# A hybrid eight-layer kernel: sparse experts whose first products run before the gate's weights, and an attention norm placed earlier in the pipeline

## The chip, the cores and the metric

The kernel runs on one core of a Trainium2 chip. A core has a matrix engine (TensorE, PE in the profile; its weight loads are PEld), a vector engine (VectorE, DVE), an engine for activation functions (ScalarE, ACT), a general one (GpSimd, POOL) and an engine that issues transfers (SyncE, SP). They run their own instruction streams in order and meet at semaphores. The metric is the device time of one execution in microseconds (us); lower is better. Times of three runs are given by their median.

## The reference

The model takes `x` of 4 batches, 1024 positions and 128 features, in float32, and applies eight layers, each to the normalised input, and each added to it:

```
x = x + _L0_attn_a_ref(_layernorm(x), ...)
x = x + _L0_ffn_ref(_layernorm(x), ...)       # sparse experts, call 1
x = x + _L0_attn_b_ref(_layernorm(x), ...)
x = x + _L0_ffn_ref(_layernorm(x), ...)       # sparse experts, call 2
x = x + _L1_attn_a_ref(_layernorm(x), ...)
x = x + _L1_ffn_ref(_layernorm(x), ...)
x = x + _L1_attn_b_ref(_layernorm(x), ...)    # multi-query attention
x = x + _L1_ffn_ref(_layernorm(x), ...)
```

Two of these matter here. The sparse experts have 8 experts of 128 hidden units, of which each token uses the best two, and a shared one that every token uses:

```
logits = einsum('btd,ed->bte', x, gate_w)
_, idx = top_k(logits + lb_bias, 2)
w = sigmoid(logits at idx);  w = w / (sum(w) + 1e-6)
we = w placed at idx, 0 elsewhere                        # token x expert
hidden = square(relu(einsum('nd,ehd->neh', x, w1)))
moe_out = sum over e of we * (hidden_e @ w2_e)
shared = square(relu(x @ cfc)) @ cproj
return moe_out + shared
```

The multi-query attention has 16 heads of 64, which share one key and one value head. Each head has a bias that depends on the distance between positions; the scores are causal:

```
q = (x @ Wq) * 64**-0.5;  k, v = x @ Wkv
sim = q k^T + 8 * rel_emb[bucket(distance)], masked above the diagonal
out = softmax(sim) v;  return out @ Wout + bout
```

## The kernel before

The stream `x_sb` stays in SBUF for the whole kernel, 128 positions to a tile, 8 tiles to a batch. Layers follow one another, and a scheduler puts the instructions of each engine in order, by their dependences and their place in the program; an inner `manual_schedule` fixes the written order for the engines it names. In the experts that is PE alone; in the multi-query attention it is PE, DVE and ACT. Work that a later layer may begin early (its norms, for instance) can be woven into the DVE and ACT streams of the layer before it.

**Sparse experts (`ffn0`, called twice).** The two batches at work at any time are objects of the class `Batch`. Its constructor normalises the batch (`layernorm`, lines 344 to 351); `turn` (L1042, L1043) transposes it on PE into `xT`; `gate` (L1019, L1050 to L1071) makes the logits on PE, and then on ACT and DVE the rank of each expert among the eight, and the weights `we` of the two best. Their square roots are taken (L1071), because the root is multiplied in ahead of the square: the square of `root * relu(h)` is `we * relu(h)^2`. Hidden units lie on partitions, so the root of each token must be the same on all 128 of them. `spread` brings this about: a transpose on PE (L1077), a copy (L1079), a write of the 64 x 128 roots to DRAM (L1081), and 16 loads that read one row into all partitions (L1087), one for each of 8 experts in each of two blocks of 512 tokens. The tile of roots has two buffers, one per block.

A `Block` is 512 tokens. `first(n)` makes the product with the first weights of one expert in a PSUM bank (L1099, two records in the trace for each matmul, with 512 columns). For the shared expert ACT rectifies it (L1102). For the other eight one DVE instruction takes the maximum with 0 and multiplies by the roots, straight from PSUM (L1105). ACT then squares the result in SBUF (L1106). `second(n)` issues a ninth of the 36 products with the second weights (L1115), which add up over the nine experts in one PSUM bank; after the ninth piece DVE adds the bank to the stream (L1124). The order on PE is that of the loop at the end of `ffn0`: for each block, nine times a `first` of this block and a `second` of the block before. The next batch is turned and gated after the seventh piece of a batch's first block, and spread after the fifth piece of its second block. There are six banks for first products, transposes and logits, and two for sums.

**Multi-query attention (`attn3`).** The loop runs over steps `s`. Each pair of heads has six steps, which take the query tiles 0 and 1, 2 and 3, 4, 5, 6, 7; a batch has eight pairs, so 48 steps. In a step, PE transposes the probabilities of the present step (L1962), makes the scores two steps ahead (L1912), which DVE biases (L1930), and ACT takes the exponentials one step ahead (L1947); then PE contracts the probabilities of the step before with the values (L1980), and after the fourth and the last tile DVE multiplies by the inverted sums (L1989). Between the two halves of the exponentials a step runs its `extras`: functions that were registered for it by `at(step, f)`. The preparation of the next batch is a list of seven such pieces, `batch.pieces`: two of statistics (`stats`, L1821 and L1822, on DVE), `scale` (a square root on ACT, L1829, which needs another function table than the exponentials, and the norm itself on POOL, L1833, eight tiles, and a bias on POOL, L1836), `turn` (L1845), `reverse` (L1852: the same tiles with the positions flipped), `keys` (L1859) and `values` (L1865). With `s` the first step of the new batch, piece `j` runs at step `s - 16 + j`: the statistics at the third and fourth step of a pair (steps are counted from 0 below, so these are steps 2 and 3), `scale` at step 4, `turn` at step 5, `reverse`, `keys` and `values` at steps 0, 1 and 2 of the next pair.

Of the kernel before, what the change touches and what calls it, by code (L numbers as in the profile page):

```python
# [29 lines left out]
AF = mybir.ActivationFunctionType  # L30
ALU = mybir.AluOpType
# [4 lines left out]
B, S, D, H = 4, 1024, 128, 16  # L36
P = 128
# [210 lines left out]
def hybrid_kernel(ctx: ExitStack, tc: tile.TileContext, x, out, blocks, dram, upto=8):  # L248
    nc = tc.nc
    mm = nc.tensor.matmul  # L250
# [32 lines left out]
    def layer_pool(name, bufs, side="left"):  # L283

        return tc.tile_pool(name=name, bufs=bufs, side=side, reuse_waits="tile")

    psum = Psum()
    bank, pair = psum.single, psum.pair
# [19 lines left out]
    early = wpool.tile([P, wide1], F32, name="wt1")  # L308
# [23 lines left out]
    after = const.tile([P, P], BF16, name="after")  # L332
# [689 lines left out]
    def ffn0(W):  # L1022

        E = 8
        with layer_pool("f0", 2, "right") as pool:

            class Batch:  # L1030
# [14 lines left out]
                def gate(self):  # L1045


                    lg = gate_logits(self.xT, W("gate"))
                    sg = small.tile([P, TB, E], F32, name="sg")
                    nc.scalar.activation(sg, lg, AF.Sigmoid)  # L1050
                    v = small.tile([P, TB, E], F32, name="v")
                    nc.vector.tensor_tensor(v, lg, wide(W("lb"), TB), ALU.add)
                    other = v.unsqueeze(2).to_broadcast([P, TB, E, E])
                    own = v.unsqueeze(3).to_broadcast([P, TB, E, E])
                    more = pool.tile([P, TB, E, E], F32, name="more", bufs=1)
                    same = pool.tile([P, TB, E, E], F32, name="same", bufs=1)
                    nc.vector.tensor_tensor(more, other, own, ALU.is_gt)
# [31 lines left out]
            class Block:  # L1089


                def __init__(self, batch, i):
                    self.batch, self.i = batch, i
                    self.hid = pool.tile([P, E + 1, 512], F32, name="hid")

                def first(self, n):
                    e = (n + E) % (E + 1)
                    ps = bank()
                    mm(ps, W("w1")[:, e * P : (e + 1) * P], self.batch.xT[:, self.i * 512 : (self.i + 1) * 512], start=True, stop=True)  # L1099
                    h = self.hid[:, e, :]  # L1100
                    if e == E:
                        nc.scalar.activation(h, ps, AF.Relu)  # L1102
                    else:
                        root = self.batch.root[self.i][:, e].rearrange("p t c -> p (t c)")
                        nc.vector.scalar_tensor_tensor(h, ps, 0.0, root, ALU.max, ALU.mult)  # L1105
                    nc.scalar.activation(h, h, AF.Square)  # L1106
# [19 lines left out]
            with tc.manual_schedule(engines={mybir.EngineType.PE}):  # L1126
                batch = Batch(0)
                batch.turn()
                batch.gate()
                batch.spread()  # L1130
                before = None
                for b in range(B):
                    for i in range(2):
                        block = Block(batch, i)
                        if i == 0 and b + 1 < B:
                            after = Batch(b + 1)
                        for n in range(E + 1):
                            block.first(n)
                            if before:
                                before.second(n)  # L1140
                            if i == 0 and n == 6 and b + 1 < B:
                                after.turn()
                                after.gate()
                            if i == 1 and n == 4 and b + 1 < B:
                                after.spread()
                        before = block
                    if b + 1 < B:
                        batch = after
                for n in range(E + 1):
                    before.second(n)  # L1150

# [634 lines left out]
    def attn3(W, table):  # L1786
# [9 lines left out]
        with layer_pool("a3", 2) as pool, layer_pool("a3k", 1) as keep:  # L1796
# [6 lines left out]
            def at(step, f):  # L1803
                extras.setdefault(step, []).append(f)
# [205 lines left out]
            for k, p in enumerate(pairs):  # L2010
                s = N * k
                for i in range(2):
                    at(s + 1 + 4 * i, lambda p=p, i=i: p.invert(i))
                    at(s + 2 + 4 * i, lambda p=p, i=i: p.spread(i))
                if k:
                    at(s - 5, p.fetch)
                    at(s - 4, p.project)
                if p.hp == 0 and k:
                    for j, piece in enumerate(p.batch.pieces):
                        at(s - 16 + j, piece)  # L2020
                if p.hp == 7:
                    for j, t0 in enumerate((0, 2)):
                        at(s + 4 + j, lambda p=p, t0=t0: p.batch.output(t0))
                        at(s + N + 1 + j, lambda p=p, t0=t0: p.batch.output(t0 + 4))
            engines = mybir.EngineType
            with tc.manual_schedule(engines={engines.PE, engines.DVE, engines.Activation}):
# [4 lines left out]
                before = None  # L2031
                for s in range(-2, total + 3):
                    p, step = (pairs[s // N], s % N) if 0 <= s < total else (None, 0)
# [18 lines left out]
                    before = (p, turned) if p else None  # L2052
# [43 lines left out]
```

## Time and profile before

| | us |
|---|---|
| median of three runs | 3670.81 (3669.97 to 3672.02) |
| the profiled execution, its own time | 3671.56 |
| its span in the trace | 3669.9 |
| experts, call 1, from its first transposes to its last second product | 920.5 to 1078.5 |
| experts, call 2, likewise | 1390.9 to 1547.1 |
| multi-query attention, from its first flips to its last output product | 2317.6 to 3424.8 |

The span is what lies between the first and the last instruction in the trace; the execution's own time has 1.66 us more around it. The page lists for each engine the time in which it was busy. A long busy share of PE does not mean that it works at its peak: its records also last longer when its clock is granted at half rate, and the page gives this clock by slices. The page's second part shows the clock below full in the first half of the kernel above all (tenths, 40 slices of 91.7 us):

```profile
PE   6999999998899998999989999999999998999999
PEclk7999999999899998989999999999999999999999
```

The trace can be asked for the instructions in a stretch in order of time, each with the idle time of its engine ahead of it and the instruction that ended this idle time. That is the view for a stretch with a few waits in it; sums over the whole span hide them.

### The profile page before, as it was taken

Reading aid. Unit: us, or ns where it says so; the run is one execution under the profiler, and the core shown is the slowest. Engines: PE = TensorE matmul, PEld = TensorE weight load, DVE = VectorE, ACT = ScalarE, POOL = GpSimd, SP = SyncE. Lnnn points to the kernel's source line nnn. Section 1 sums busy time; section 2 is a strip of 40 time slices with the busy share of each in tenths; the row PEclk is TensorE's granted clock in tenths of the full one; section 3 lists DMA queues with packets and bytes.
Section 4 is the critical chain, followed back from the end, with each engine's and each line's share of the span. In section 5 each row is a group of like instructions: output and inputs, shape, how many; then the busy total and the mean of one; then the engine's idle time right before and its main releaser. Section 6 shows DMA issues by size and latency. Waiting matters only on the chain.

```text
span 3669.9 us, 62785 instructions
## 1 busy us (share of the span) xinstructions
PE 3474.5 (95%) x25672; PEld 2046.2 (56%) x25672; DVE 2068.1 (56%) x4938; ACT 1961.9 (53%) x3349; POOL 919.0 (25%) x706
## 2 busy tenths in 40 slices
PE   6999999998899998999989999999999998999999
PEld 3344444435574556633333477666766766766777
DVE  5666666666653445468778621466566566566311
ACT  5455555556432223367767654466566566566543
POOL 4677777783004210122221100001001001000000
PEclk7999999999899998989999999999999999999999
DMA  3111111100430003400000000111001001010000
GB/s 99 46 47 47 47 47 47 47 24 1 139 87 1 1 1 108 116 1 1 1 1 1 14 1 1 61 34 36 27 33 36 28 32 35 24 36 24 4 9 13
DMA packets 95978, 124.36 MB, mean 34 GB/s; under 512 B 3660, under 2 KB 78028, under 8 KB 94536
## 3 DMA queue, kind: packets, MB, share of 16 engines
q1 hardware_dynamic: 95688, 120.33, 10.7%
q8 instruction: 202, 3.31, 0.4%
q14 instruction: 88, 0.72, 0.1%
HBM read 117.59 MB, written 2.73 MB: 33 GB/s over the span
## 4 chain that ended last, share of the span: by engine, by line
PE 83%; DVE 7%; ACT 6%; POOL 2%; issue 1%; DMA 1%; SPq 0%; ACTq 0%; DVEq 0%; POOLq 0%
PE mm L1962 8%; PE s L1912 8%; PE av L1749 6%; PE mm L1739 6%; PE av L1980 6%; PE s L734 5%; PE s L701 4%; PE s L1584 4%; PE av L772 3%; PE av L1115 3%; PE mm L1099 3%; PE av L1618 3%; ACT p L1947 2%; DVE p L1595 2%; PE mm L1288 2%; PE av L1324 2%
## 5 line engine op out<-in xcount | busy, mean ns | idle before, releaser
L764 POOL TENSOR_TENSOR p<-p,bias 128x1536 f32<-128x1536 f32 x192 | 504.3, 2627 | 89.0 <-ACT p L746 78.3
L1930 DVE CUSTOM_DVE_ANT_0 p<-s,bias 128x512 f32<-128x512 f32 (+3 forms) x768 | 387.2, 550 | 131.2 <-PE s L1912 123.9
L715 DVE TENSOR_REDUCE parts<-s 128x2 f32<-128x1024 f32 (+4 forms) x384 | 350.0, 953 | 151.5 <-PE s L701 90.6
L1947 ACT ACTIVATE p<-p,tops 128x128 f32<-128x128 f32 (+7 forms) x512 | 395.2, 774 | 2.7 <-DVE tops L1930 1.9
L1595 DVE TENSOR_SCALAR p<-s 128x1024 f32<-128x1024 f32 (+1 forms) x320 | 340.8, 1111 | 92.8 <-PE s L1584 83.5
L1967 ACT COPY pt<-mm 128x512 f32<-128x512 f32 (+1 forms) x352 | 185.8, 528 | 369.1 <-PE mm L1962 369.0
L1962 PE MATMUL mm<-ident,p 128*128 128x128 f32 x2304 | 348.7, 284 | 36.3 <-ACT p L1947 32.5
L1962 PEld LDWEIGHTS mm<-ident,p 128*128 128x128 f32 x2304 | 249.6, 141 | 173.4 <-issue 64.7
L1598 ACT ACTIVATE p<-p 128x2048 f32<-128x2048 f32 (+1 forms) x160 | 277.6, 1740 | 96.4 <-DVE p L1595 95.8
L1749 PEld LDWEIGHTS av<-wt,hid 128*128 128x128 f32 x2048 | 263.9, 192 | 107.1 <-issue 107.1
L1995 POOL COPY wide_rec<-rec 128x512 f32<-128x512 f32 x64 | 39.4, 616 | 1121.1 <-DVE rec L1993 1118.6
L1912 PE MATMUL s<-keys,q 64*128 64x512 f32 (+3 forms) x1536 | 303.6, 514 | 4.0 <-DVE tops L1930 4.0
L743 ACT ACTIVATE p<-s 128x1024 f32<-128x1024 f32 x192 | 155.7, 811 | 271.2 <-PE s L734 264.9
L1980 PE MATMUL av<-pt,vals 128*64 128x128 f32 x4608 | 295.1, 277 | 0.0
L1740 ACT ACTIVATE hid<-mm,wt 128x512 f32<-128x512 f32 x256 | 170.7, 690 | 220.8 <-PE mm L1739 220.5
L1980 PEld LDWEIGHTS av<-pt,vals 128*64 128x64 f32 x4608 | 248.8, 137 | 49.6 <-issue 38.5
L1749 PE MATMUL av<-wt,hid 128*128 128x128 f32 x2048 | 264.7, 275 | 0.0
L1739 PE MATMUL mm<-xT,wt 128*128 128x512 f32 x512 | 261.8, 602 | 2.5 <-ACT hid L1740 2.0
L1969 DVE COPY pt<-mm 128x512 f32<-128x512 f32 (+1 forms) x288 | 189.6, 658 | 131.8 <-PE mm L1962 131.7
L734 PE MATMUL s<-q,k 32*128 32x512 f32 (+3 forms) x1536 | 227.9, 537 | 0.5 <-DVE parts L715 0.5
L1584 PE MATMUL s<-q,k 32*128 32x512 f32 (+3 forms) x1536 | 213.5, 542 | 2.1 <-DVE p L1595 1.7
L701 PE MATMUL s<-k,q 32*128 32x512 f32 (+3 forms) x1280 | 180.3, 513 | 10.3 <-DVE parts L715 6.9
(400 smaller groups left out, 5281.0 us busy)
## 6 DMA issues: line engine op xcount, KB each, us to landing
root<-roots SPq DMA_DIRECT2D x128, 256.0 KB, 6.4
bias<-rel_dram SPq DMA_DIRECT2D x32, 1024.0 KB, 5.5
bias<-pos_dram SPq DMA_DIRECT2D x16, 1536.0 KB, 7.0
bias<-pos_dram SPq DMA_DIRECT2D x16, 512.0 KB, 7.9
wt<-w_ffn SPq DMA_DIRECT2D x2, 2132.0 KB, 8.1
wt<-w_ffn SPq DMA_DIRECT2D x2, 1192.0 KB, 5.3
wt<-w_attn SPq DMA_DIRECT2D x1, 2336.0 KB
x_sb<-x SPq DMA_DIRECT2D x4, 512.0 KB, 6.9
```

What stands on the lines that cost most here:

```text
L715: nc.vector.tensor_reduce(o, x, AX.X, ALU.max, negate=True)
L734: mm(both[h // 2][:, h % 2, 0:w], self.k[jt // 4][r, (3 - jt % 4) * P : (4 - jt % 4) * P], self.q[i][r, w0:512], start=True, stop=True,)
L764: nc.gpsimd.tensor_tensor(d, d, self.bias[:, 0:3, u : u + w], ALU.mult)
L1584: mm(both[h // 2][:, h % 2, c : c + 512 - w0], self.k[r, jt * P : (jt + 1) * P], self.q[r, 512 * i + w0 : 512 * (i + 1)], start=True, stop ...
L1595: nc.vector.tensor_scalar(pt[:, 2 * hp : 2 * hp + 2, 0:w], both[hp][:, :, 0:w], 80.0, -80.0, ALU.min, ALU.max)
L1739: mm(ps, W("w1")[:, c * P : (c + 1) * P], self.batch.xT[:, self.i * 512 : (self.i + 1) * 512], start=True, stop=True)
L1749: mm(o, self.hid[:, c, t * P : (t + 1) * P], W("w2")[:, c * P : (c + 1) * P], start=(c == 0), stop=(c == C - 1))
L1912: mm(s[:, kk, 0:e], self.q[r, it * P : (it + 1) * P], keys[self.n][r, S - n + c : S - n + c + e], start=True, stop=True,)
L1930: nc.vector.tensor_tensor_reduce(out=self.p[it][:, kk, c : c + e], in0=s[:, kk, 0:e], in1=self.bias[:, kk, c : c + e], scale=-1.0, scalar= ...
L1947: nc.scalar.activation(p, p, AF.Exp, bias=self.top[it][:, kk : kk + 1], scale=-1.0, accum_out=self.sums[:, it, kk : kk + 1])
L1962: nc.tensor.transpose(ps[:, m, kk, :], self.p[it][:, kk, (m0 + m) * P : (m0 + m + 1) * P], ident)
L1980: mm(self.acc[64 * kk : 64 * kk + 64, (it % 4) * P : (it % 4 + 1) * P], vals[self.n][:, it - m0 - m, :], pt[:, m, kk, :], start=(m0 + m == 0),
```

## The change

Two things are changed.

In `ffn0` the first batch's 18 first products (two blocks of nine) get their own two functions. `early` makes the product and rectifies it on ACT, for all nine experts, without roots. `weigh` multiplies the eight experts' results by the roots in SBUF, on DVE, and squares them on ACT. The written order becomes: turn and gate the first batch; nine `early` of block 0; `spread`; nine `early` of block 1; turn and gate the second batch; `weigh` all of both blocks; the 36 second products of block 0, now with no first products between them; `spread` of the second batch. From the second batch on the loop is that of before, with the second block of the first batch as the block before.

In `attn3` the seven pieces run at steps `s` less 21, 20, 19, 13, 11, 9 and 8 instead of 16 to 10. The statistics and `scale` are thus five steps earlier (steps 3, 4 and 5 of an earlier pair), `turn` stays, and `reverse`, `keys` and `values` come at steps 1, 3 and 4 of the pair in which they were at 0, 1 and 2.

The operations of every other layer, and their order on each engine, are as before. So is the number of instructions on PE, DVE, POOL and SP; ACT has 32 more, 16 in each call of `ffn0`.

```diff
+                def early(self, n):
+
+                    e = (n + E) % (E + 1)
+                    ps = bank()
+                    mm(ps, W("w1")[:, e * P : (e + 1) * P], self.batch.xT[:, self.i * 512 : (self.i + 1) * 512], start=True, stop=True)
+                    nc.scalar.activation(self.hid[:, e, :], ps, AF.Relu)
+
+                def weigh(self, n):
+                    e = (n + E) % (E + 1)
+                    h = self.hid[:, e, :]
+                    if e < E:
+                        root = self.batch.root[self.i][:, e].rearrange("p t c -> p (t c)")
+                        nc.vector.tensor_tensor(h, h, root, ALU.mult)
+                    nc.scalar.activation(h, h, AF.Square)
+
...
                 batch.gate()
-                batch.spread()
-                before = None
-                for b in range(B):
+                early = [Block(batch, i) for i in range(2)]
+                for i in range(2):
+                    for n in range(E + 1):
+                        early[i].early(n)
+                    if i == 0:
+                        batch.spread()
+                after = Batch(1)
+                after.turn()
+                after.gate()
+                for i in range(2):
+                    for n in range(E + 1):
+                        early[i].weigh(n)
+                for n in range(E + 1):
+                    early[0].second(n)
+                after.spread()
+                before = early[1]
+                for b in range(1, B):
+                    batch = after
                     for i in range(2):
...
                             block.first(n)
-                            if before:
-                                before.second(n)
+                            before.second(n)
...
                 if p.hp == 0 and k:
-                    for j, piece in enumerate(p.batch.pieces):
-                        at(s - 16 + j, piece)
+
+                    for j, piece in zip((21, 20, 19, 13, 11, 9, 8), p.batch.pieces):
+                        at(s - j, piece)
```

More of the change, by code (lines that the diff above doesn't have):

```diff
@@ L1146, in ffn0 @@
                         before = block
-                    if b + 1 < B:
-                        batch = after
                 for n in range(E + 1):
```

## Prediction

> **What bounds the kernel now.** I read the page first: one engine holds the span.
>
> ```profile
> span 3669.9 us, 62785 instructions
> PE 3474.5 (95%) x25672; PEld 2046.2 (56%) x25672; DVE 2068.1 (56%) x4938; ACT 1961.9 (53%) x3349; POOL 919.0 (25%) x706
> root<-roots SPq DMA_DIRECT2D x128, 256.0 KB, 6.4
> ```
>
> TensorE (PE) is busy 95%. The change issues every matmul of before and no other, so it can win only where PE stands still or runs at a reduced clock. I then read the timeline at the head of both expert layers (calls 1 and 2) and at the three places in the multi-query layer where the next batch is prepared. Head of call 1 (columns: start, length, engine, line, operands; in brackets the idle time before and its releaser):
>
> ```profile
> 922.60 3.50 PE L1019 MATMUL mm<-wt,xT 128*128 128x8 f32 x16
> 932.23 0.26 ACT L1071 ACTIVATE we<-we 128x64 f32<-128x64 f32 x1 [4.35 <-DVE we L1070]
> 932.54 0.42 PE L1077 MATMUL mm<-ident,we 128*64 128x128 f32 x1 [6.44 <-ACT we L1071]
> 932.76 7.92 PE L1099 MATMUL mm<-xT,wt 128*128 128x512 f32 x14
> 935.18 16.27 SPq L1087 DMA_DIRECT2D root<-roots  x16
> 940.27 1.53 DVE L1105 SCALAR_TENSOR_TENSOR hid<-mm,root 128x512 f32<-128x512 f32 x2 [5.49 <-DMA root<-roots]
> ...
> 969.12 1.02 PE L1099 MATMUL mm<-xT,wt 128*128 128x512 f32 x2
> ```
>
> PE ends the gate logits at 926.1 and waits 6.44 us for the gate chain of VectorE (DVE) and ScalarE (ACT). Then seven first products fill the PSUM banks, and PE waits again, for DVE, which waits for the roots from DRAM. The row at 969.12 is the second batch's first product. From there on both kernels issue the same PE work, so this instant ("the meeting point") measures the head. Call 2 has the same rows: gate end 1395.57, roots' transpose 1401.96, first multiply 1409.65, meeting point 1437.73.
>
> The clock, by windows of 5 us (PE, PEld, DVE, ACT, POOL busy; granted clock; DMA share; GB/s):
>
> ```profile
> 930.00:935.00 5.00, 2.46 (x4) 1.23 (x5) 4.51 (x27) 0.76 (x3) 0.00 (x0) 0.50 0.03 7
> 935.00:940.00 5.00, 5.00 (x11) 2.10 (x10) 0.00 (x0) 0.94 (x2) 0.00 (x0) 0.87 0.34 97
> 955.00:960.00 5.00, 5.00 (x31) 3.69 (x30) 4.28 (x11) 1.54 (x4) 0.00 (x0) 1.00 0.06 9
> ```
>
> After the idle stretch the clock is 0.50. The 14 records at 932.76 would last 14 x 0.43 = 6.0 us at full clock (0.43 is their later spacing) and last 7.92, so 1.9 us is lost; in call 2 they last 8.73, a loss of 2.7.
>
> In the multi-query layer a pair of heads lasts 31.3 us by its last VectorE product (2410.21 to 2441.81 and on). Around the first and second preparation two pairs (2492.68 to 2566.00, 2767.31 to 2840.85) take 10.7 and 10.9 more, of which the prepared products are 6.9 (1.23 + 1.95 + 1.88 + 1.89). Around the third it is 16.7 (3010.85 to 3121.50, less three pairs). First and third:
>
> ```profile
> 2512.74 1.28 ACT L1829 ACT_TABLE_LOAD   x1
> 2514.59 6.24 POOL L1833 TENSOR_SCALAR xn<-x_sb,ln_mv,ln_rs 128x128 f32<-128x128 f32 x8 [17.32 <-DVE ln_rs L1830]
> 2516.85 1.75 PE L1962 MATMUL mm<-ident,p 128*128 128x128 f32 x7 [2.87 <-ACT p L1947]
> ...
> 3067.55 0.99 PE L1962 MATMUL mm<-ident,p 128*128 128x128 f32 x7 [3.05 <-ACT p L1947]
> 3071.57 0.64 DVE L345 BATCH_NORM_AGGREGATE ln_mv<-ln_st 128x2 f32<-128x6 f32 x8 [5.74 <-POOL xn L1833]
> 3074.63 1.11 PE L1962 MATMUL mm<-ident,p 128*128 128x128 f32 x4 [3.80 <-DVE pt L1969]
> ```
>
> PE waits for exponentials that stand behind the square root and its two table loads (1.28 + 0.21 + 1.28). In the third preparation the last layer's norms are woven in: one more square root at 3067.5, and DVE stands 5.74 us for GpSimd (POOL), with PE behind it.
>
> **Experts, part by part** (once per call, two calls).
> - Removed: 16 fused multiplies from PSUM (L1105, 0.69 each) and their dependence of the first products on the roots. Added: 16 rectifications on ACT (the shape of L1102, 0.60) and 16 multiplies in SBUF on DVE. No row shows just these; the nearest, L1060, a product of two 128x512 tensors in SBUF, takes 0.64 to 0.69, both ends equal to what is removed. The 9.6 us on ACT lie under first products that take 0.86 us each on PE; bare, they would be on the path.
> - Moved: the nine first products of block 0 go ahead of the roots' transpose, those of block 1 behind it, with nothing between them waiting for roots.
>
> The chain in call 1: gate end 926.1, nine first products 9 x 0.86 = 7.7, and a slow clock. The gate products already run at 0.50, so I charge the 1.9 us of the row above (bounds: 0 if the gate keeps the clock up, 3.8 if it rises twice as late). The transpose comes at 935.7 instead of 932.5. The roots' chain (transpose, copy, DRAM, sixteen loads) keeps its rows: 7.7 us to the first multiply, then 15 steps of 16.27 / 16 = 1.02, 15.3. Now the new wait: the second batch's gate is interleaved on DVE with block 1's multiplies, and its square root on ACT stands behind all squares; PE cannot go on to the meeting point without it. After the last landing come a multiply 0.69, a square 0.63, a table load 1.28, a root 0.26 and the transpose, with gaps 3.3. Meeting point: 935.7 + 7.7 + 15.3 + 3.3 = 962.0, against 969.1: 7.1 saved.
>
> Call 2: 1395.57 + 7.7 + 2.7 = 1406.0 (the gate's own chain is ready at about 1405.5, because ACT now does three rectifications ahead of the norm's root that DVE waits for); + 26.3 = 1432.3 against 1437.7: 5.4 saved. Bounds: clock never low, 17.2 for both calls; twice as slow and once more slow at the restart, 3.4.
>
> PE's own work is the second chain. Behind ACT's two squares of the first landed roots (strict order in the ACT stream) wait three rectifications and the copies of the second batch's transposes, so its gate ends near 951, and 36 second products (0.22 each, 7.9, plus 2 at low clock) reach 961. Two chains of equal length: the saving can be no larger without both moving. Behind the meeting point the second batch's roots are issued later relative to their use: first multiply near 969.7, while PE needs that bank back for the next transposes, seven pairs of 1.755 later, at 974.3. Cover 4.6 us; if it is gone, the excess is stall.
>
> [...]
>
> **Multi-query attention.** The norm's square root goes from step 4 of a pair, amid the 1024-wide exponentials, to step 5 of an earlier pair, amid those of the first two tiles. An undisturbed pair shows the cover there: ACT's exponentials end at 2425.2 and PE transposes at 2425.30 with no wait. Putting 2.8 us of table loads and root ahead delays PE by about 3.0, where 2.87 goes. The 6.24 us on POOL was hidden before and stays so; the flips, keys and values are as long at their new steps. First two preparations: 0 (bounds: 1.5 us of clock each, either way). Third: the two further square roots now come one step apart. Stepping through ACT (each further one 1.28 + 0.21 + 1.28, against PE's 4.9 us a step) I get PE 5.7 us late in all, where the first kind is 4.5 late; so 1 to 2 us over the first kind, where it was 6.0. Saved 4 (bounds: 9, if all low-clock stretches vanish too, and -3, if the 5.7 us wait for POOL hits the next tile's scores).
>
> **Sum.** 7.1 + 5.4 + 4 = 16.5 off the profiled execution's 3671.56 (its span 3669.9 plus 1.66 around it): 3655.1. That execution is 0.75 above the median of the runs, 3670.81, so 3654.
>
> **Rivals.**
> - Slow clock: the head saves less, because PE goes slow again in its gaps (2.9 us idle before the second gate). For it: 0.50 to 0.65 over much of 920 to 950. Against: the next 27 products run without a gap. Both calls save 3.4 to 7: 3660 to 3664.
> - The roots take the head's place (slower): everything at the meeting point hangs on the last of sixteen loads, and behind it on the next sixteen. At a spacing above 1.5 us instead of 1.02 a call loses; at 2.0 (the longest issue of that line is 2.5) the calls lose 7.6 and 9.3, 3684 in all with the attention's 4 saved. Against: both calls show 1.02, and the weights' transfer that could collide is done before 930.
> - The attention's move only shifts its stall, and costs: POOL's 6.24 holds DVE ahead of the next biased scores in the third preparation. -3 instead of 4: 3661.
> - Nothing in the heads: PE's second chain is longer than I make it, up to 969. Then 3667.
>
> **How the numbers follow.** No change means within 0.2%, 7.3 us, about what a measurement of this kernel can tell. Forecast 0.56; slow clock 0.18; attention's loss alone 0.08; nothing in the heads 0.08; roots 0.10. Faster: 0.56 + 0.15 + 0.07 = 0.78; same: the rest of those two and nothing in the heads, 0.12; slower 0.10. Range: from all bounds good (17.2 + 9 = 26 saved, 3645) to the heads at their worst bound with nothing from the attention (3667).
>
> **What would show it.** Head of call 1: the 6.44 wait after the gate gone, transpose near 935.7, meeting point near 962 and 1432 less what call 1 saved. A wait of ACT's root (L1071's like) ahead of the second batch's transpose. At the preparations one wait of about 3 us at step 5 instead of 4; the third with 10.7 to 13 us over two regular pairs instead of 16.7. I am wrong if the meeting points don't move, or if stalls for roots stand behind them.

## The result, and the profile after

The changed kernel takes 3657.36 us (median of six runs, 3655.5 to 3662.41) against 3671.89 for the kernel before on the same chip (six runs, 3669.97 to 3681.38): a ratio of 0.9961, 95% interval 0.995 to 0.9971. That is 14.5 us, 0.4%. The profiled execution of the changed kernel took 3658.74. Its page, the lines that answer to those shown of before:

```profile
span 3657.0 us, 62759 instructions
PE 3477.7 (95%) x25672; PEld 2049.5 (56%) x25672; DVE 2066.3 (57%) x4938; ACT 1978.0 (54%) x3381; POOL 919.3 (25%) x706
root<-roots SPq DMA_DIRECT2D x128, 256.0 KB, 6.5
```

PE issues the same 25672 matmuls and ACT has 32 more instructions. PE's busy time did not fall, it rose by 3 us: 12.9 us of span went, all of it out of PE's waits. Where they went, by instants that both traces have:

| instant | before | after | gained up to there |
|---|---|---|---|
| call 1, first transposes | 920.54 | 922.45 | -1.9 |
| call 1, meeting point | 969.12 | 966.75 | 2.4 |
| call 2, first transposes | 1390.90 | 1388.55 | 2.4 |
| call 2, meeting point | 1437.73 | 1430.84 | 6.9 |
| multi-query attention, last VectorE product of its first pair | 2367.14 | 2361.42 | 5.7 |
| the same, of its last pair | 3417.54 | 3404.32 | 13.2 |
| end of the span | 3669.9 | 3657.0 | 12.9 |

So the two heads gave 4.3 and 4.5 in this pair of profiles and the attention 7.5; the first layer, unchanged, happened to be 1.9 slower, and the stretch from call 2's meeting point to the attention's first pair 1.2.

The head of call 1 after (timeline, columns as before; L1101 is the early product, L1109 the multiply by the roots, L1131 the second product, L1115 the pipelined first product that stands at the meeting point):

```profile
927.86 10.98 PE L1101 MATMUL mm<-xT,wt 128*128 128x512 f32 x18
938.68 0.27 PE L1078 MATMUL mm<-ident,we 128*64 128x128 f32 x1
946.31 0.69 DVE L1109 TENSOR_TENSOR hid<-hid,root 128x512 f32<-128x512 f32 x1 [6.20 <-DMA root<-roots]
950.17 2.87 PE L1019 MATMUL mm<-wt,xT 128*128 128x8 f32 x16 [2.62 <-ACT xT L1044]
952.90 10.62 PE L1131 MATMUL av<-wt,hid 128*128 128x128 f32 x72
966.31 0.26 ACT L1072 ACTIVATE we<-we 128x64 f32<-128x64 f32 x1
966.62 0.30 PE L1078 MATMUL mm<-ident,we 128*64 128x128 f32 x1 [3.10 <-ACT we L1072]
966.75 1.02 PE L1115 MATMUL mm<-xT,wt 128*128 128x512 f32 x2
```

The 6.44 us wait behind the gate is gone: the early products start at the gate's end. PE now waits 2.62 us for the second batch's transposed input and 3.10 us for that batch's rooted weights. The 18 early records at 927.86 would last 7.7 at full clock and last 10.98. The windows of 5 us show why (last three columns: granted clock, DMA share, GB/s):

```profile
925.00:930.00 5.00, 5.00 (x18) 3.97 (x18) 4.00 (x24) 3.39 (x6) 0.00 (x0) 0.50 0.77 323
930.00:935.00 5.00, 5.00 (x8) 1.96 (x8) 5.00 (x22) 2.16 (x4) 0.00 (x0) 0.61 0.00 0
955.00:960.00 5.00, 5.00 (x34) 5.00 (x34) 3.91 (x7) 2.33 (x5) 0.00 (x0) 0.72 0.91 242
```

What ends the head is on VectorE. Its timeline, from the ninth of the sixteen multiplies (L1058 to L1071 are the second batch's gate chain):

```profile
956.09 0.69 DVE L1109 TENSOR_TENSOR hid<-hid,root 128x512 f32<-128x512 f32 x1 [1.59 <-DMA root<-roots]
956.70 0.68 DVE L1058 TENSOR_TENSOR more<-v 128x512 f32<-128x512 f32 x1
...
963.65 0.69 DVE L1109 TENSOR_TENSOR hid<-hid,root 128x512 f32<-128x512 f32 x1
964.25 0.20 DVE L1070 RECIPROCAL tot<-tot 128x8 f32<-128x8 f32 x1
...
964.57 0.22 DVE L1071 TENSOR_TENSOR we<-we,tot 128x64 f32<-128x64 f32 x1
```

After 956.09 no multiply waits for a root: VectorE is simply full for 8.7 us with multiplies and gate chain alternating. The last roots were not far ahead, though: the last load was issued at 957.00, and those of this head whose landing is recorded took 5.9 to 7.6 us, so an estimate from these puts it at 962.9 at the earliest, for a multiply at 963.65. In call 2 the last root does come last (VectorE's last multiply there waits 0.23 us for its transfer, at 1427.72).

Multi-query attention, first and third preparation after (timeline; L1857 is the norm's root, L1861 its normalisation on GpSimd, L1975 the exponentials):

```profile
2481.00 1.28 ACT L1857 ACT_TABLE_LOAD   x1
2482.52 1.28 ACT L1975 ACT_TABLE_LOAD   x1
2482.85 6.27 POOL L1861 TENSOR_SCALAR xn<-x_sb,ln_mv,ln_rs 128x128 f32<-128x128 f32 x8 [1.30 <-DVE ln_rs L1858]
2484.36 1.04 PE L1990 MATMUL mm<-ident,p 128*128 128x128 f32 x5 [2.12 <-ACT p L1975]
...
3031.37 1.04 PE L1990 MATMUL mm<-ident,p 128*128 128x128 f32 x5 [2.95 <-ACT p L1975]
3036.13 0.64 DVE L345 BATCH_NORM_AGGREGATE ln_mv<-ln_st 128x2 f32<-128x6 f32 x8 [5.21 <-POOL xn L1861]
3039.90 1.56 PE L1940 MATMUL s<-keys,q 64*128 64x512 f32 x8 [1.36 <-DVE tops L1958]
```

The wait is at its new step, and at the first two preparations it is 2.12 us where it was 2.87 and 3.05. At the third it is 2.95, and VectorE still stands 5.2 us for GpSimd.

### The profile page after: what moved, and what is told of

The parts are those of the page before. It is cut to its first block, busy times and chain, and to the rows that moved or that the text cites. A ratio compares the mean times of both kernels' runs of the same rounds, so it can differ in the third digit from the quotient of the medians.

```text
span 3657.0 us, 62759 instructions
## 1 busy us (share of the span) xinstructions
PE 3477.7 (95%) x25672; PEld 2049.5 (56%) x25672; DVE 2066.3 (57%) x4938; ACT 1978.0 (54%) x3381; POOL 919.3 (25%) x706
## 4 chain that ended last, share of the span: by engine, by line
PE 83%; DVE 6%; ACT 6%; POOL 2%; issue 1%; DMA 1%; SPq 1%; ACTq 0%; DVEq 0%; POOLq 0%
PE mm L1990 8%; PE s L1940 8%; PE av L1777 6%; PE mm L1767 6%; PE av L2008 6%; PE s L734 5%; PE s L701 4%; PE s L1612 4%; PE av L772 3%; PE av L1646 3%; PE av L1131 3%; PE mm L1115 2%; ACT p L1975 2%; DVE p L1623 2%; PE mm L1316 2%; PE av L1352 2%
## 5 line engine op out<-in xcount | busy, mean ns | idle before, releaser
L1975 ACT ACTIVATE p<-p,tops 128x128 f32<-128x128 f32 (+7 forms) x512 | 395.2, 774 | 2.3 <-DVE tops L1958 2.1
L2023 POOL COPY wide_rec<-rec 128x512 f32<-128x512 f32 x64 | 39.4, 616 | 1163.1 <-DVE rec L2021 1098.9
```

What stands on the lines that cost most here:

```text
L1975: nc.scalar.activation(p, p, AF.Exp, bias=self.top[it][:, kk : kk + 1], scale=-1.0, accum_out=self.sums[:, it, kk : kk + 1])
```

## The experiments

Two measures recur. The head: from its first transposes to its meeting point. A preparation: the time of the four pairs around it, by VectorE's last product of a pair; before, the three took 142.93, 143.16 and 148.95 us, after 141.21, 141.22 and 145.40. Runs of the kernel before stood beside each group, and ratios are to these.

**Each part alone.** The experts alone: the changed kernel with the old steps of the seven pieces.

```diff
-                    for j, piece in zip((21, 20, 19, 13, 11, 9, 8), p.batch.pieces):
-                        at(s - j, piece)
+                    for j, piece in enumerate(p.batch.pieces):
+                        at(s - 16 + j, piece)
```

> The change of the experts alone; the attention's preparation stands where it stood before. Theory A, read from the trace of the changed kernel: each head saves 4.3 to 4.5 us, so 8.8 in all, near 3663, and the multi-query attention lasts as long as before (1050.4 us between the last VectorE products of its first pair and of its last). Rival B, the terms of the prediction: 12.5, near 3659. If the two edits help or hinder each other, this and the run with the attention's edit alone do not add up to the 14.5 of both.

Measured: 3664.21 (six runs) against 3674.25 (fifteen), ratio 0.9969, 0.9958 to 0.998. The heads take 41.6 and 40.7 us, 7.0 and 6.2 less than in the profile before; the attention's preparations 143.07, 141.62 and 148.76. The 10.0 us by the medians lie between theory A's 8.8 and rival B's 12.5 and decide for neither.

The attention alone: the kernel before, with the new line of the diff above in place of the old one.

> The attention's edit alone; the experts as before. Theory A: 7.5 us saved, near 3664: 1.7 to 1.9 at each of the first two preparations, because the wait of 2.1 us is too short to bring the clock down as the 2.9 us of before did, and 3.6 at the third. Rival B, the prediction: nothing at the first two and 4 at the third, near 3668.

Measured: 3666.47 (nine runs), ratio 0.9976, 0.9966 to 0.9986. Preparations 141.21, 141.21 and 145.34, as in the changed kernel to 0.1 us; the heads 47.7 and 44.7, as before. Theory A holds: 7.8 us by the medians. Each part works by itself, in its own place. By the medians the parts give 10.0 and 7.8, 17.8 together.

**Which part of the attention's move.** First only the norm and its statistics moved, with flips, keys and values at the old steps:

```diff
-                    for j, piece in zip((21, 20, 19, 13, 11, 9, 8), p.batch.pieces):
+                    for j, piece in zip((21, 20, 19, 13, 12, 11, 10), p.batch.pieces):
```

> The changed kernel, but flips, keys and values stand at 12, 11 and 10 steps ahead as before; only statistics and norm are five steps earlier. Theory A: the saving comes from where the square root stands, so the three preparations last as in the changed kernel (141.2, 141.2 and 145.4 us over four pairs with the outputs), within 0.5. Rival: spreading out flips, keys and values gives it; then 142.9, 143.2 and 148.9 as before.

Measured, one run: 3650.99. Preparations 141.12, 141.12 and 146.93, the wait 2.12 again. The norm's move is what saves; the three other pieces are worth nothing at the first two preparations and at most 1.5 us at the third (four later profiles with all seven pieces at the new steps last 147.0 there too). Then the norm early, but at the kind of step where it was before (step 4, amid the widest exponentials):

```diff
-                    for j, piece in zip((21, 20, 19, 13, 11, 9, 8), p.batch.pieces):
+                    for j, piece in zip((22, 21, 20, 13, 11, 9, 8), p.batch.pieces):
```

> The changed kernel, but statistics and norm are one step earlier still (22, 21, 20), so the square root stands at the fourth step of a pair, counted from 0, as it did before the change, only a pair earlier. Theory A: the kind of step decides; PE waits 2.9 us instead of 2.1 and its clock falls, so the first two preparations last 142.7 to 143.2 over four pairs instead of 141.2. Rival: it is being earlier that helps (GpSimd's 6.3 us of norm no longer sit next to the transposes that need them); then 141.2.

Measured, one run: 3664.29; preparations 143.16, 144.39 and 148.38, and PE waits 2.87 us as before. Being earlier saves nothing; the kind of step does.

**Is it the length of the wait, through the clock?** The changed kernel, with ScalarE copies that nothing reads behind the norm's root: one in the first preparation, two in the second.

```diff
                     nc.scalar.activation(rs, rs, AF.Sqrt)
+                    for _ in range(self.b if self.b < 3 else 0):
+                        idle = pool.tile([P, 512], F32, name="idle", bufs=1)
+                        nc.scalar.copy(idle.rearrange("p (t d) -> p t d", t=4), self.x[:, 0:4, :])
                     nc.vector.reciprocal(rs, rs)
```

> The changed kernel with one unread ScalarE copy of 128x512 (about 0.6 us) behind the norm's square root in the first of the three preparations of the multi-query layer, two of them in the second, none in the third: TensorE's wait at the new step grows from 2.1 us to about 2.7 and 3.3. Theory A (the change saves more than its bare wait because 2.1 us do not lower the clock and 2.9 do): the first preparation, 141.21 us over four pairs, grows by more than the copy, by about 2.3 (0.6 and 1.7 at a low clock), the second by 2.9 to 3.1, with windows of granted clock under 1 behind the wait. Rival (the clock's windows fall otherwise; the length of the wait does not decide): the first grows by 0.6 and the second by 1.2, at full clock. The third stays at 145.4 to 147.0.

The waits of PE at the two preparations (timeline):

```profile
2481.71 1.04 PE L1993 MATMUL mm<-ident,p 128*128 128x128 f32 x5 [2.63 <-ACT p L1978]
2482.68 1.35 PE L1943 MATMUL s<-keys,q 64*128 64x512 f32 x8
...
2755.83 1.04 PE L1993 MATMUL mm<-ident,p 128*128 128x128 f32 x5 [3.28 <-ACT p L1978]
2756.81 2.41 PE L1943 MATMUL s<-keys,q 64*128 64x512 f32 x8
```

The eight score products behind the wait take 1.35 us after 2.63 and 2.41 after 3.28. One run, 3658.66. Preparations: 141.75, which is 0.54 more than in the changed kernel, a little more than the wait's 0.51; and 143.92, 2.70 more, of which the longer wait is 1.16 and the remaining 1.54 a clock of 0.50 in the stretch from 2757 to 2760. The first half of theory A's forecast failed (2.63 did not lower the clock), the second held. The other profiles say how much the length decides. A wait of 2.12 us stands at the first two preparations of ten profiles (after, and nine of the experiments), and all twenty last 141.1 to 141.2. One of 2.87 to 3.06 stands there in three (before, the experts alone, the norm early at the old kind of step): five of the six last 142.9 to 144.4, and one, the second of the experts alone, waits 3.05 us, keeps its clock and lasts 141.62. So a longer wait costs the clock more often, but its length does not decide alone; the last section shows from the same profiles what does.

**Does the slow clock at the start of the head cost anything?** The changed kernel with seven unread products ahead of the first batch's transposes, in call 1 only:

```diff
+        def fill(k):
+            ps = bank()
+            for _ in range(k):
+                mm(ps, W("w1")[:, 0:P], W("w1")[:, 0:512], start=True, stop=True)
...
+                if not calls:
+                    fill(7)
+                calls.append(1)
                 batch.turn()
```

> The changed kernel with seven further 128x512 products (nothing reads them) ahead of the first batch's transposes in the first head only, where TensorE stands still; they keep the granted clock up, and otherwise cost nothing as long as they fit into that wait. Theory A (the head still loses time to a slow clock, 3.2 us over the first 18 early records in the profile of after): the 18 records last about 7.8 us instead of 10.98, the roots' transpose comes about 3 us earlier counted from the first transpose, and the first head's meeting point too by up to 3, unless VectorE's queue takes some of it back; the second head does not move. Rival (the clock costs nothing at the end of the head, VectorE's sixteen multiplies and the gate chain set it): the transpose comes earlier, the meeting point by less than 1 us.

```profile
913.84 6.17 PE L1028 MATMUL mm<-wt 128*128 128x512 f32 x14
920.91 2.20 PE L1050 MATMUL mm<-ident,xn 128*128 128x128 f32 x8 [0.90 <-DVE xn L351]
922.90 3.43 PE L1019 MATMUL mm<-wt,xT 128*128 128x8 f32 x16
926.18 9.69 PE L1108 MATMUL mm<-xT,wt 128*128 128x512 f32 x18
```

The wait of 6.90 us ahead of the transposes is 0.90 now, and yet the gate's products run at half clock (3.43 for what takes 1.95 at full clock) and the early ones take 9.69. The clock fell at 922.9, with the transposes, which come as slowly as VectorE delivers their input (2.20 us where eight in a row take 1.04). From the first transposes to the roots' transpose it is 14.94 us, no better than in five profiles of this order without the fill (14.6 to 14.9) and 1.3 better than in two (16.2, 16.3). One run, 3659.45. The fill does not do what it was meant to; the head takes 42.0 us, where the profiles without the fill have 41.0 to 44.3. Whether a faster clock here would shorten the head it cannot say.

**What ends the head.** The changed kernel with block 1's multiplies behind the second batch's gate. The column of ones is computed from that batch's rooted weights, so that they cannot go ahead of them:

```diff
-                for i in range(2):
-                    for n in range(E + 1):
-                        early[i].weigh(n)
+                one = small.tile([P, 1], F32, name="one")
+                nc.vector.tensor_scalar(one, after.we[:, 0, 0:1], 0.0, 1.0, ALU.mult, ALU.add)
+                for n in range(E + 1):
+                    early[0].weigh(n)
...
                 after.spread()
+                for n in range(E + 1):
+                    early[1].weigh(n, one)
```

> The changed kernel with the eight multiplies of block 1 put behind the second batch's gate chain and square root (by one further operand, a column of ones computed from that batch's rooted weights; it costs one small VectorE operation in each call). Theory A (the first batch's multiplies on VectorE and squares on ScalarE stand ahead of the second gate and set the meeting point): the meeting point comes earlier, bounded then by TensorE's own second products, about 3 us in the first head and 2 in the second, some 5 us in all, about 3652. Rival (TensorE's second chain ends as late anyway, as the prediction has it): the meeting points stay within 1 us and the time within 2 us of the changed kernel's in this batch; or, if the late multiplies of block 1 hold its second products, TensorE stalls there and it is slower by the up to eight multiplies of 0.69 us.

```profile
949.89 10.34 PE L1134 MATMUL av<-wt,hid 128*128 128x128 f32 x72
960.07 0.27 PE L1078 MATMUL mm<-ident,we 128*64 128x128 f32 x1
960.18 1.02 PE L1118 MATMUL mm<-xT,wt 128*128 128x512 f32 x2
...
963.13 2.05 PE L1134 MATMUL av<-wt,hid 128*128 128x128 f32 x8 [0.18 <-ACT hid L1113]
```

PE no longer waits for the rooted weights: its second products run into their transpose without a gap, and the meeting point is 38.0 us behind the first transposes (44.3 in the profile after, 41.0 to 44.3 in seven profiles of the changed order). In call 2 it is 39.4, where that order has 38.5 to 42.3. A little comes back: the next second products wait for the late squares, 2.05 us instead of 1.05. The time is 3654.63 (five runs, 3653.37 to 3656.95), ratio 0.9947, 0.9934 to 0.9959; the changed kernel, run again beside it:

> The changed kernel once more, beside the two versions above on the same chip. Theory A (both parts save independently; each alone measured 0.9969 and 0.9976): product 0.9945, about 20 us below the kernel before; the first measurement, 0.9961 with 0.995 to 0.9971, was low by chance of the clock's phase. Rival (the parts overlap or one takes back from the other): again 0.996, 14 to 15 us.

3659.77 (five runs, 3652.05 to 3666.5), ratio 0.9956, 0.9942 to 0.9969. By the medians the reordering is 5.1 us faster than the changed kernel, but the intervals overlap, so of these two the faster one is likely, not settled. Both beat the kernel before. As to the parts: 0.9956 again lies nearer to the first measurement than to the product of the two parts, 0.9945, but the interval holds both.

With fills besides, seven as above in call 1 and three ahead of the second gate's products in both calls:

```diff
+                fill(3)
                 after.gate()
```

> The kernel with block 1's multiplies behind the second gate, and besides seven unread 128x512 products ahead of the first batch's transposes in the first call and three ahead of the second batch's gate products in both calls, where TensorE waits. Theory A (what is left in the heads is the slow clock after TensorE's waits): the 36 second products last 7.9 us instead of 10.0 to 10.6, and the heads (first transposes to meeting point) are 3 to 5 us shorter than with the reordering alone in the first call, 1 to 2 in the second; about 3647. Rival (nothing left but the roots' chain): the same time as the reordering alone within 2 us, with the extra products seen at the path's cost.

```profile
949.03 1.81 PE L1141 MATMUL av<-wt,hid 128*128 128x128 f32 x14
951.82 0.49 PE L1141 MATMUL av<-wt,hid 128*128 128x128 f32 x2 [0.97 <-ACT hid L1120]
953.87 8.14 PE L1141 MATMUL av<-wt,hid 128*128 128x128 f32 x56 [1.56 <-ACT hid L1120]
```

3654.62 (3652.27 to 3665.28), ratio 0.9952, 0.9938 to 0.9966: no gain over the reordering alone. The heads take 39.5 and 37.1 us. The second products do start faster, and catch up with what they multiply: they wait 0.97 us for a square whose multiply waited 1.08 us for its root, and 1.56 us for a square that stands behind the second gate's table load and sigmoid on ScalarE (951.78 to 953.29). Behind the slow clock stand the roots' chain and ScalarE's queue.

**A wait elsewhere that differs from profile to profile.** Between the two calls lies an attention layer that the change does not touch, and the way through it, from the meeting point of call 1 to the first transposes of call 2, took 421.8 us in some profiles of the kernels before and changed and up to 433.9 in others. Up to 5.5 us of the difference arise at its head, in the same instructions. The timelines of the changed kernel and of the kernel with reordering and fills, third and fourth group of the products of its weights:

```profile
1085.37 1.16 PE L1201 MATMUL mm<-wt,wT 128*128 128x128 f32 x8 [2.71 <-DVE wT L1198]
1088.20 1.16 PE L1201 MATMUL mm<-wt,wT 128*128 128x128 f32 x8 [0.78 <-DVE wT L1198]
```

```profile
1084.72 2.07 PE L1218 MATMUL mm<-wt,wT 128*128 128x128 f32 x8 [2.71 <-DVE wT L1215]
1089.28 2.08 PE L1218 MATMUL mm<-wt,wT 128*128 128x128 f32 x8 [0.78 <-DVE wT L1215]
```

The wait is 2.71 us both times; behind it the products take 1.16 in the one and 2.07 in the other, and the clock stays at 0.50 for 17 us. Take the stretch from the third group of centring products (`mm<-centre,wt`, L1196 after) to the first gathering product (`t<-kt,xn`, L1274): it lasts 18.1 us at clock 1.00 in seven of the first ten profiles, and 22.3 to 23.6 with a spell at 0.50 in the other three (the attention alone, the changed kernel again, reordering with fills). The expectation below counts five and five, and from 20.8; the traces show seven and three. Three attempts to fill that wait, the first with five unread products in the changed kernel:

```diff
                 nc.vector.tensor_copy(wT, ps)
+                if n == 2:
+                    ps = bank()
+                    for _ in range(5):
+                        mm(ps, W("wqkv")[:, 0:P], W("wqkv")[:, 0:512], start=True, stop=True)
                 ps = bank()
```

> The changed kernel with five unread 128x512 products (2.15 us) at the head of the attention layer behind each expert layer, where TensorE waits 2.71 us for VectorE's copy. In ten profiles the stretch from the third group of centring products to the first gathering product there, the same instructions each time, lasted 18.1 us in five of them (clock 1.00) and 20.8 to 23.6 in the other five (clock 0.50 to 0.60). Theory A (that wait decides whether the clock falls, and this is most of what differs between runs of one kernel): the stretch lasts 18.1 to 18.5, and the runs lie closer together than the 14.5 us of the changed kernel's last five, with a median 2 to 5 us lower. Rival (the clock falls there for another reason): the stretch is again long in some layers, and spread and median stay.

Measured: 3660.05 (six runs, 3658.17 to 3664.47), ratio 0.9967, 0.9955 to 0.9979. The same with the reordering:

> Both the reordering of block 1's multiplies behind the second gate and the five unread products of the run beside it. Theory A: the two savings add, 3 to 5 us for the heads and 2 to 5 for the wait in the attention layer, near 3650 and the fastest of all versions. Rival: no faster than the reordering alone, 3654.6.

Measured: 3657.43 (five runs, 3656.96 to 3657.93), ratio 0.9959, 0.9947 to 0.9972. The size was wrong: a 128x512 product is two records, so five take 4.46 us and not 2.15, longer than the wait. One group later a new wait stands, 3.09 and 3.10 us, the clock falls, and the stretch takes 25.9 in both. With two products, which fit:

```diff
-                    for _ in range(5):
+                    for _ in range(2):
```

> The reordering of block 1's multiplies behind the second gate, with two unread 128x512 products instead of five in TensorE's wait of 2.71 us (a product of that shape is two records of 0.43, so two are 1.7 us and stay inside the wait, where five, 4.5 us, overran it and a new wait of 3.1 us stood one group later). Theory A (the wait's length decides whether the clock falls there): what is left of the wait is about 1 us, no other wait grows, the stretch lasts 18.1 us at clock 1.00, and the time is at or under the reordering's 3654.6, near 3652, with a spread of a few us. Rival (the clock falls there whatever the wait, or the extra products move VectorE's and GpSimd's work so that another wait takes its place): the stretch lasts over 20 us and the time stays at 3655 to 3658.

Measured: 3659.42 (five runs, 3656.09 to 3662.42), ratio 0.9966, 0.9952 to 0.998; of the 2.71 us wait 1.00 is left, but the new one behind the next group is there again with 3.06, and the stretch takes 21.3. The rival holds: the extra work shifts PE against VectorE, and another wait takes the place of the one that was filled. All three are slower than, or no faster than, their parents by the medians. Whether this wait makes most of the spread between runs stays open: the three kernels whose one profile has the new wait have runs 6.3, 1.0 and 6.3 us apart, the changed kernel's last five lie 14.5 apart, which fits, but the reordering alone, with the old wait, has 3.6, which does not; and a spread of five runs is a weak measure.

## Why the prediction was right, and where not

It said 3654 within 3645 to 3667 and faster by over 0.2%; 3657.36 and 0.4% came. Its sum was 16.5 us off the profiled execution; the profiled executions differ by 12.8, the medians by 14.5. That it came so near is partly luck: in the profile after the heads gave 8.8 where 12.5 were forecast and the attention 7.5 where 4 were, two misses that cancel to 16.3 in all; the 3.4 us by which the whole is lower were lost in stretches that nobody had changed.

*The heads, 7.1 and 5.4: right in size, by an average over profiles.* The lengths in all profiles with the written order of before or of the change (the fill left out in call 1):

| head | before (2 profiles) | changed order | predicted |
|---|---|---|---|
| call 1 | 48.6, 47.7 | 44.3, 43.3, 41.7, 41.6, 41.4, 41.2, 41.0; mean 42.1 | 41.5 |
| call 2 | 46.8, 44.7 | 42.3, 41.8, 41.5, 41.2, 40.7, 39.8, 39.7, 38.5; mean 40.7 | 41.4 |

The means differ by 6.1 and 5.1. The profile after alone shows 4.3 and 4.5; its call 1 is the longest of seven. The charge for the slow clock, 1.9 and 2.7, is 3.2 and 2.7 in that profile (10.98 and 10.48 for what takes 7.74 at 0.43 each). In the profile before the granted clock rises from 0.50 to 1.00 3.7 us behind the roots' transpose in call 1 and 5.4 in call 2. Over seven profiles the roots' transpose comes 15.2 us behind the first transposes in call 1, where the prediction has 15.2.

*The wait behind the gate, the rows of the roots, the place of the new wait: right.* PE goes straight from the gate to the early products; the first multiply is 7.6 behind the roots' transpose in both calls (7.7 predicted); the new wait is for ScalarE's root, as forecast.

*"15 steps of 1.02, then 3.3" as what sets the head's end: near in size, but only one of two bounds.* In call 2 of the profile after the first multiply is at 1411.18, the last at 1427.72, 16.5 later (15.3 predicted), and it waits for its root. In call 1 it is 17.3, no multiply after the ninth waits for its root, and the sixteen multiplies with the gate chain among them fill VectorE. Of the sixteen heads of this order in eight profiles VectorE waits for one of the last two roots in five, by 0.2 to 1.0 us, and for none after the ninth in eleven. The step that failed is the one that priced the multiplies as equal to those removed: they are, and the prediction names the gate chain that is interleaved with them, but it puts the cost of that queue at nothing, where the reordering shows some 3 us.

*"Two chains of equal length: the saving can be no larger without both moving": wrong.* PE's own chain ends at 963.5 and waits 3.1 more; in the sixteen heads of this order it waits 1.1 to 3.5. The reordering moved only the other chain, and in the three profiles with it and no further fill in the head call 1 takes 38.0, 40.1 and 39.4 us (mean 39.2 against 42.1), call 2 39.4, 36.8 and 37.9 (38.1 against 40.7).

*Attention, 0 for the first two preparations and 4 for the third: too low for the two, about right for the third.* Saved were 1.7, 1.9 and 3.6; in four profiles with this preparation unchanged the third is at 147.0, where 1.9 is saved. The step that failed is "delays PE by about 3.0, where 2.87 goes". The wait is 2.12, because ScalarE is ahead of PE there: without the 2.81 us of loads and root the first exponentials would have ended at 2481.5 (2484.31 less 2.81), and PE comes for them at 2482.2 (2484.36 less 2.12). And it does not lower the clock, which 2.87 and 3.05 did. Of the 1.7 and 1.9 saved, 0.75 and 0.93 are the shorter wait, and the 1.0 that is left of each is the clock, inside the bound of 1.5 named there "either way". The lengthened wait fits: at 3.28 us, 1.54 of clock are back.

*The rivals.* The slow clock came in part: both heads of the profile after saved 8.8 together, between this rival's 7 and the forecast's 12.5. The roots did not take the head's place: their spacing stayed near 1.1. The attention did not lose. The bank that PE needs back at the second turn was free in time: the first multiply there is at 972.96, the turn at 979.02.

*One reading of the prediction is a little off, and the sum does not hang on it.* The products at 2410.21 and 2441.81 are those after the fourth tile of their pairs, 31.6 apart; by the last product a regular pair lasts 31.3, as said there.

## What to carry to other kernels

When a wait is filled with work that was due later, look at what this work needs next on the other engines: here the multiplies were no dearer, but they stood in one queue with the chain that the next stage waits for, and putting that chain ahead of half of them shortened the heads by a further 2.9 and 2.6 us on average, of which a part came back behind them. A wait of PE cost its length here and sometimes a slow clock behind it, so cutting one from 2.87 to 2.12 us saved 1.7 us at the first preparation, more than the 0.75 that was cut; whether it does so depends on where the wait falls, as the next section shows. And before a single profile is taken as the measure of a stretch, see how far the same instructions differ between profiles: here by up to 5.5 us in one stretch that nobody had changed.

## What the runs showed of the hardware

*Waits of one length that lower the clock in one execution and not in the next.* The granted clock takes two values, 0.50 and 1.00, in all fourteen profiles. If the windows of the view are made narrow around its changes, they lie on a grid of 3.41 us in each profile (in the profile after, for one, down at 3033.12 and up at 3036.53), and a slow spell lasts one or several steps of it (3.41 us in the lines below, 17.07 at the attention's head of the kernel with reordering and fills). From profile to profile the grid stands elsewhere against the kernel's instructions.

So a wait can be laid on the grid of its profile. Three sorts of wait were: that at the attention's head (14 profiles), those of the first two preparations (28), and those for the rooted weights at the meeting points of the changed order (16). Length does not tell which of them lower the clock: 2.71 us at the attention's head did in three of eleven profiles, 3.10 at call 1's meeting point in the profile after did not. The longest part of the wait that lies in one step of the grid does:

| longest part of the wait in one step of 3.41 us | waits | clock falls at that step's end |
|---|---|---|
| up to 1.84 us | 37 | 0 |
| 1.90 to 2.00 us | 6 | 3 |
| 2.05 us or more | 15 | 15 |

The 2.12 us of the changed preparation were cut by the grid in all twenty cases, so that at most 1.77 lay in one step; why the grid stood so alike there is not shown. A wait of that length is not safe everywhere. In the third preparation of the experts alone, one of 2.13 us lay wholly in one step, and the clock fell at its end (timeline, then windows, third column from the right the granted clock):

```profile
3064.62 0.66 PE L1990 MATMUL mm<-ident,p 128*128 128x128 f32 x4 [2.13 <-DVE pt L1997]
```

```profile
3061.73:3065.15 3.42, 1.29 (x11) 0.95 (x10) 3.38 (x14) 1.18 (x2) 2.21 (x1) 1.00 0.00 0
3065.15:3068.56 3.41, 3.21 (x22) 2.50 (x21) 3.04 (x10) 1.97 (x5) 0.61 (x1) 0.50 0.02 5
```

The lengthened waits fit: 2.63 us had 1.38 in one step and kept the clock, 3.28 had 2.31 and lost it. In these 58 waits, then, 2.05 us or more without a product in one step went with a lower clock at its end in all fifteen cases, also where PE was busy in the rest of the step (in the first preparation of the profile before for 0.74 us, with 2.67 of the wait). Outside the three sorts the length of the part does not settle it: the wait of 2.95 us in the third preparation of the profile after lay with 1.29 and 1.66 in two steps, and the clock fell at the second one's end (granted clock 1.00 from 3029.80 to 3033.10, 0.50 from 3033.15 to 3036.50). What decides there, and why the clock follows such a grid, no run here shows.

*A VectorE operation that lasts as long as a GpSimd one beside it.* That 2.71 us wait has a likely cause. VectorE and GpSimd in the profile after:

```profile
1080.47 3.39 DVE L351 TENSOR_SCALAR xn<-x_sb,ln_mv,ln_rs 128x128 f32<-128x128 f32 x5
```

```profile
1080.89 2.38 POOL L1243 TENSOR_TENSOR x_sb<-x_sb,wt 128x1024 f32<-128x1024 f32 x1 [206.64 <-DVE xn L351]
```

Five normalisations take 1.36 us elsewhere in this stretch (1077.63) and 3.39 here, 2.03 more: one of them, started at 1080.98, takes 2.37 us where the others take 0.34, while GpSimd's add of 128x1024 runs from 1080.89 to 1083.27; VectorE's next operation starts at 1083.78, and the copy that PE waits for stands behind it. The profile before has the same: five normalisations in 3.39 us from 1082.83, and the add in 2.38 from 1083.25. That the add holds the normalisation up is the author's estimate from these times; what the two engines would have to share for it the profile does not show, and no run here moved that add.
